# A soft mixture-of-experts layer: slot logits in three single-pass products instead of seven float32 products of halves

## The chip, the core and the metric

The kernel runs on one core of one Trainium2 chip as one program. The metric is device microseconds of that core from launch to end: 1880.38 us, the median of 3 runs (1880.1 to 1885.45). A core has a matrix engine (PE, with its weight loads PEld), a vector engine (DVE), an activation engine (ACT), a general engine (POOL), a sequencer that issues transfers (SP), an on-chip memory SBUF, and an accumulator memory PSUM that PE writes and DVE and ACT read. Each engine works through its own queue in order and waits on semaphores.

## The reference, cut to what matters

Four layers follow each other, each a graph convolution and a feed-forward part, on 625 nodes with 768 features. The change is in the feed-forward part of the third, `L2_ffn`, a soft mixture of 4 experts with 1024 slots each:

```python
x = x + _L2_ffn_ref(_layernorm(x, axis=-1)[None], phi, w1, b1, w2, b2)[0]

def _L2_ffn_ref(x, phi, w1, b1, w2, b2):
    logits = jnp.einsum('bnd,esd->bnes', x, phi)
    B, N, E, S = logits.shape
    dispatch = jax.nn.softmax(logits, axis=1)
    combine = jax.nn.softmax(logits.reshape(B, N, E * S), axis=-1).reshape(B, N, E, S)
    slots = jnp.einsum('bnd,bnes->besd', x, dispatch)
    h = jax.nn.gelu(jnp.einsum('besd,edh->besh', slots, w1) + b1[None, :, None, :])
    y = jnp.einsum('besh,ehd->besd', h, w2) + b2[None, :, None, :]
    return jnp.einsum('besd,bnes->bnd', y, combine)
```

The logits are one product of 4096 x 768 (phi) with 768 x 625 (x transposed). All inputs and outputs are float32.

## The kernel before

Nodes lie in 5 tiles of 125 (`TILES`), features in 6 blocks of 128 (`KD`). `x` (125 x 5 x 768) and the normalized, transposed `xT` (128 x 6 x 625, with a 626th column of zeros in `xTp`) stay in SBUF from stage to stage. Weights come through a pool `w` of 4 buffers, each filled by one transfer that SP issues (`weight`, L151). PSUM gives 4 tiles of 1024 columns in turn (`ps`, L89). The program is built by a scheduler that orders each engine's queue by dependences and priorities, so the order of the source is not quite the order of the queues.

`L2_ffn` has three parts.

First, x times w1 for the four experts, into `xw` (125 x 5 x 768): tile 0 by itself, then two pairs of tiles by `tile_pair`, which makes a 2 x 2 block product from seven block products (`right_sums` on DVE, `left_sums` on POOL). The last node tile is only normalized and turned while this runs (`turn_due`, called in `whole`). The bias row `br` is added on POOL (L1958).

Second, 16 *fronts*, `front(i)`, each making the logits of 256 slots (two blocks of 128) for all 625 nodes. phi is loaded 512 slots at a time. `half_nodes` makes sums of halves of xT once (DVE, partly in the place of xT). For each front `half_products` makes four sums of 128 x 384 from phi on POOL (L340 to L344), one front ahead, and `half_mm` runs seven products of halves, each 3 matmuls with 128 weight columns and 313 moving columns in float32; the results are combined by seven adds on DVE (L360) and one copy on ACT (L368). The two logit blocks of a front form a `pair` (128 x 2 x 625). `largest_slots(i)` then takes each slot's maximum over nodes, the exponentials `ex`, and the running maximum `M` over slots.

Between the products of a front other work of PE is interleaved by the three lists `c`: `turn` (five transposes of `ex`, copied from PSUM to `Dn` by DVE and ACT in alternation, `copy` L106) and `hidden` (five matmuls of `Dn` with `xw`, scaled on DVE into `hE`), both for the slots of the front before. In the second front after an expert's last one, `spread` puts the node maxima into `mrow`, `weights` subtracts them from the expert's four pairs on DVE (L1799) and takes exponentials on ACT (L1802), and `combine` multiplies the pairs with `hE` on PE (80 records) into `Z`, which lies where `xw` lay. So up to six pairs live at a time (`ltp`, 6 buffers).

Third, after the fronts, the last expert is finished, `Z` is scaled, turned and multiplied with w2 (`turn_sums`, `out`), and `out` adds the result to `x[:, t]` and hands the tile on to the next layer (`final`).

Of the kernel before, what the change touches and what calls it, by code (L numbers as in the profile page):

```python
# [8 lines left out]

F32 = mybir.dt.float32  # L10
BF16 = mybir.dt.bfloat16
F16 = mybir.dt.float16
I32 = mybir.dt.int32
AF = mybir.ActivationFunctionType
ALU = mybir.AluOpType
AX = mybir.AxisListType

N = 625
P = 125
NT = N // P  # L20
D = 768
KD = D // 128
# [2 lines left out]
FF = 192  # L25
NF = NEXP * FF // 128
BIG = 1e30
TILES = [slice(t * P, (t + 1) * P) for t in range(NT)]


def halves(r):

    return r.rearrange("p (h c) -> p h c", h=2)


class Net:
# [310 lines left out]
    def half_mm(self, pool, prods, top, bottom, between=((), (), ())):  # L347


        nc, HN, HK = self.nc, self.HN, self.HK  # L350
        pa, pb = self.ps(), self.ps()
        a1, a2 = pa[:, 0:HN], pa[:, 512 : 512 + HN]
        b1, b2 = pb[:, 0:HN], pb[:, 512 : 512 + HN]

        def prod(n, to):
            A, B = prods[n - 1]
            self.mm(to, [A[:, k, :] for k in range(HK)], [B[:, k, :] for k in range(HK)])

        def add(out, in0, in1):
            nc.vector.tensor_tensor(out, in0, in1, ALU.add)  # L360

        C11, C12, C21, C22 = (
            c[:, n] for c in (top, bottom) for n in (slice(0, HN), slice(HN, N))
        )
        U2 = pool.tile([128, HN], F32, tag="U2", name="U2", bufs=1)
        U3, w = C21, N - HN
        prod(1, a1)
        nc.scalar.copy(C11, a1)  # L368
        prod(6, a2)
        add(U2, C11, a2)  # L370
        prod(7, b1)
        add(U3, U2, b1)
        prod(5, b2)
        add(C22, U3[:, 0:w], b2[:, 0:w])
        add(C12, U2[:, 0:w], b2[:, 0:w])
        for f in between[0]:
            f()
        prod(4, a1)
        add(C21, U3, a1)
        for f in between[1]:  # L380
            f()
        prod(2, a2)
        add(C11, C11, a2)
        for f in between[2]:
            f()
        prod(3, b1)
        add(C12, C12, b1[:, 0:w])

    def half_begin(self, pool, prods, top):

# [1264 lines left out]
    def L2_ffn(self):  # L1655
        nc, tc, a, x = self.nc, self.tc, self.a, self.x
        NE, HF, NB = 4, 192, 8
        with ExitStack() as ctx:
            big = ctx.enter_context(tc.tile_pool(name="f2", bufs=1))


# [2 lines left out]
            f = big.tile([P, NT, NE], F32, name="f")  # L1664
# [3 lines left out]
            nc.gpsimd.memset(fp, 0.0)  # L1668
            with ExitStack() as c1:
                b1 = c1.enter_context(tc.tile_pool(name="f2e", bufs=1))  # L1670
                xw = b1.tile([P, NT, NE, HF], F32, name="xw")
                Z = xw
                xT = self.xT


                br = self.row(None, D, a["L2_ffn_b1"].rearrange("(o e) f -> o (e f)", o=1))
                ws = []
                for j in range(2):
                    w = self.wp.tile([128, KD, 2, HF], F32, tag="w", name="w1")
# [7 lines left out]
                with tc.tile_pool(name="f2x", bufs=1) as xp:  # L1687

                    ws = [w.rearrange("p k e f -> p k (e f)") for w in ws]
                    pv = self.hv(self.ps(), P)  # L1690
                    for j in range(2):
                        self.mm(
                            pv[:, j, :], [xT[:, k, TILES[0]] for k in range(KD)],
                            [ws[j][:, k, :] for k in range(KD)],
                        )
                    nc.vector.tensor_tensor(halves(xwf[0]), pv, halves(br), ALU.add)
                    HK = self.HK
                    rights = self.right_sums(
                        xp, [[w[:, k : k + HK, :] for w in ws] for k in (0, HK)]
                    )  # L1700
                    lefts = {1: self.left_sums(xp, xT, 1, inplace=False)}

                    def whole():
                        self.turn_due(NT - 1)
                        lefts[3] = self.left_sums(xp, xT, 3, inplace=False)

                    for t in (1, 3):
                        self.tile_pair(
                            xp, lefts[t], rights,
                            [xwf[o][:, js] for o in (t, t + 1) for js in (slice(0, 384), slice(384, D))],  # L1710
                            whole if t == 1 else None,
                        )
                ltp = c1.enter_context(tc.tile_pool(name="f2l", bufs=6))
                mp = c1.enter_context(tc.tile_pool(name="f2m", bufs=1))
                tp = c1.enter_context(tc.tile_pool(name="f2t", bufs=2))
                pairs, hEs, Ms, S = {}, {}, {}, {}
                ph, sts, exs, Dns, rows = {}, {}, {}, {}, {}

                B = self.half_nodes(b1, inplace=True)

                def sums_of_phi(i):
                    g, j = divmod(i, 2)
                    if j == 0:
                        ph[g] = self.weight(
                            a["L2_ffn_phiT"][:, g * 512 : (g + 1) * 512], KD, 512
                        )
                    S[i] = self.half_products(tp, B, ph[g], *(
                        slice((2 * j + o) * 128, (2 * j + o + 1) * 128) for o in range(2)
                    ))

                def front(i, *between):

                    pair = pairs[i] = ltp.tile([128, 2, N], F32, tag="lt", name="lt")
                    self.half_mm(tp, S.pop(i), pair[:, 0, :], pair[:, 1, :], between)

                def largest_slots(i):

                    e, q = divmod(i, NB // 2)
                    pair = pairs[i]
                    for o in range(2):  # L1740
                        st = sts[2 * i + o] = self.small.tile(
                            [128, 3], F32, tag="sm2", name="sm2", bufs=5
                        )
                        lt = pair[:, o, :]
                        nc.vector.tensor_reduce(st[:, 0:1], lt, AX.X, ALU.max, negate=True)
                        ex = exs[2 * i + o] = tp.tile([128, N], F32, tag="ex", name="ex")
                        nc.scalar.activation(
                            ex, lt, AF.Exp, bias=st[:, 0:1], accum_out=st[:, 1:2]
                        )
                    if q == 0:  # L1750
                        M = Ms[e] = mp.tile([128, N], F32, tag="M", name="M")
                        nc.vector.tensor_tensor(M, pair[:, 0, :], pair[:, 1, :], ALU.max)
                    else:
                        for o in range(2):
                            nc.vector.tensor_tensor(Ms[e], Ms[e], pair[:, o, :], ALU.max)

                def turn(i):
                    tv = self.nv(self.ps(), P, 128)
# [123 lines left out]
                def turn_sums(t, ks):  # L1882

                    if t not in zTs:
                        zT = ltp.tile([128, NK + 1, P], F32, tag="lt", name="zT")
                        zTs[t] = zT[:, 0:NK, :]
                        fTs[t] = zT[:96, NK, :].bitcast(BF16)[:, 0:P]
                    n = len(ks)
                    pv = self.ps()[:, 0:1024].rearrange("p (k c) -> p k c", c=128)[:, :, :P]
                    z = Z[:, t].rearrange("p e f -> p (e f)")  # L1890
                    for i, k in enumerate(ks):
                        nc.tensor.transpose(
                            pv[:, i, :], z[:, k * 128 : (k + 1) * 128], self.ident[:P, :P]
                        )
                    if ks[-1] < NK - 1:
                        nc.scalar.copy(zTs[t][:, ks[0] : ks[-1] + 1, :], pv[:, 0:n, :])
                        return
                    nc.scalar.copy(zTs[t][:, ks[0] : ks[-1] + 1, :], pv[:, 0:n, :])
                    nc.tensor.matmul(
                        pv[:96, n, :], fp[:, t].rearrange("p j r -> p (j r)"),  # L1900
                        self.identb[:P, :P], start=True, stop=True,
                    )
                    nc.vector.tensor_copy(fTs[t], pv[:96, n, :])

                def out(t, ks):
# [15 lines left out]
                            )  # L1921
                    if not last:
                        return
                    xv = halves(x[:, t, :])
                    nc.vector.scalar_tensor_tensor(
                        xv, pv, rs[:, t : t + 1], xv, ALU.mult, ALU.add
                    )
                    self.final(t)

# [29 lines left out]
                for i in range(LAST):  # L1959
# [14 lines left out]
                    if i == LAST - 1:  # L1974

                        turn(o)
                        turn(o + 1)
                    largest_slots(i)
                    if e >= 0 and q == 0:
                        largest(e)  # L1980
                    if e >= 0 and q == 1:
# [447 lines left out]
```

## Time and profile before

| What | Value |
|---|---|
| median of 3 runs | 1880.38 us |
| span of the profiled execution | 1877.8 us |
| mean granted PE clock | 0.985 of full |
| `L2_ffn`, 995.2 to 1394.0 us of the span | 398.8 us |
| of it x times w1, up to 1030.4 | 35.2 us, PE busy all of it |
| of it the fronts, up to 1322.9 | 292.5 us |
| of it the rest | 71.1 us, PE busy 67.94 |

The profiled execution is one run; its span goes from the first instruction to the last and lies 2.6 us under the median of the timed runs. In the timeline, a line is a group of like instructions: start, length, engine, line of the source, operation, tiles out<-in, shape and count, and in brackets how long the engine was idle before it and what ended that. A float32 matmul leaves two records, a float32 transpose one. The length of a PE record goes to the end of the pipeline, so successive records overlap; the time a matmul takes is read from start to start. The groups of sums that the change removes, over the fronts alone:

```
L340 POOL TENSOR_TENSOR S<-w 128x384 f32<-128x384 f32 x14 | 14.3, 1018 | 163.5 <-PE ps L125 163.5
L341 POOL TENSOR_TENSOR S<-S,w 128x384 f32<-128x384 f32 x14 | 14.0, 1001 | 1.1
L343 POOL TENSOR_TENSOR w<-w 128x384 f32<-128x384 f32 x14 | 21.9, 1564 | 0.0
L344 POOL TENSOR_TENSOR S<-w,S 128x384 f32<-128x384 f32 x14 | 19.8, 1414 | 0.0
```

Behind the count stand busy us and mean ns of one, then the idle time of the engine before them.

### The profile page before, as it was taken

What the parts mean: (1) busy time and instruction counts of PE and PEld (TensorE: products, weight loads), DVE (VectorE), ACT (ScalarE), POOL (GpSimd) and SP (SyncE); (2) the same over time, 40 slices, a digit from 0 to 9 for tenths busy, and PEclk for the clock granted to TensorE, in tenths of its full rate; (3) what the DMA queues carried; (4) which work ended last, traced back from release to release, by engine and by line L of the source; (5) the groups of instructions that cost most, each with busy time, mean ns of one, the idle gap of its engine ahead of it and who ended that gap; (6) DMA issues with size and microseconds to landing.
All of it is one profiled execution on the core that took longest, in us unless ns stands there. A gap on an engine that the chain in (4) does not pass through costs nothing.

```text
span 1877.8 us, 21626 instructions
## 1 busy us (share of the span) xinstructions
PE 1816.6 (97%) x8224; PEld 1268.2 (68%) x8224; DVE 1132.1 (60%) x2253; ACT 525.1 (28%) x950; POOL 649.7 (35%) x496
## 2 busy tenths in 40 slices
PE   8868899999999999999999999999999999999998
PEld 7835566556677766655555788878767888556765
DVE  8799856658566765675836464554756555144452
ACT  2468721002254533110110131322314333111200
POOL 0068665335410045743206322231235321401551
PEclk9959899999999999999999999999999999999999
DMA  2040033211200024414421211001011111021321
GB/s 70 25 143 34 19 110 99 79 59 36 87 22 26 1 70 150 132 51 148 135 67 37 73 62 40 26 26 34 6 40 46 39 63 67 1 80 46 99 68 33
DMA packets 69637, 115.03 MB, mean 61 GB/s; under 512 B 8189, under 2 KB 38111, under 8 KB 69534
## 3 DMA queue, kind: packets, MB, share of 16 engines
q1 hardware_dynamic: 69274, 113.57, 18.9%
q8 instruction: 65, 1.06, 0.2%
q14 instruction: 38, 0.31, 0.1%
q10 hardware_dynamic: 260, 0.09, 0.0%
HBM read 111.63 MB, written 2.01 MB: 61 GB/s over the span
## 4 chain that ended last, share of the span: by engine, by line
PE 86%; DVE 7%; ACT 3%; DMA 2%; issue 1%; SPq 0%; ACTq 0%; DVEq 0%
PE ps L125 68%; PE ps L118 3%; PE ps L1543 2%; PE ps L1575 2%; PE ps L1914 2%; PE ps L781 2%; DVE gat_w L595 2%; PE ps L1562 2%; DVE junk L575 2%; PE ps L189 1%; PE ps L1760 1%; DMA x<-in_x 1%; PE ps L132 1%; PE ps L719 1%; DVE av_junk L1380 1%
## 5 line engine op out<-in xcount | busy, mean ns | idle before, releaser
L340 POOL TENSOR_TENSOR S<-w 128x384 f32<-128x384 f32 x40 | 42.0, 1054 | 383.8 <-PE ps L125 281.7
L125 PE MATMUL ps<-xT,w 128*128 128x313 f32 x480 | 137.6, 427 | 0.7 <-ACT pr L1551 0.7
L565 POOL TENSOR_TENSOR gat_w<-gat_w,xT 125x625 f32<-125x625 f32 x60 | 86.1, 1469 | 119.7 <-DVE xT L537 97.6
L125 PE MATMUL ps<-w,xT 128*125 128x384 f32 (+2 forms) x392 | 125.3, 473 | 0.0
L125 PE MATMUL ps<-T,w 128*128 128x313 f32 x408 | 122.0, 430 | 0.8 <-DVE U L414 0.8
L125 PEld LDWEIGHTS ps<-xT,w 128*128 128x128 f32 x480 | 89.2, 189 | 33.6 <-ACT pr L1551 0.9
L125 PE MATMUL ps<-T,S 128*128 128x313 f32 x348 | 103.7, 431 | 1.7 <-DVE T L320 1.4
L125 PEld LDWEIGHTS ps<-w,xT 128*125 128x125 f32 x392 | 72.8, 188 | 46.4 <-issue 11.3
L125 PE MATMUL ps<-xT,S 128*128 128x313 f32 x336 | 100.8, 429 | 0.0
L125 PE MATMUL ps<-w,S 128*125 128x384 f32 x292 | 99.2, 486 | 0.0
L125 PEld LDWEIGHTS ps<-T,w 128*128 128x128 f32 x408 | 75.6, 189 | 31.9 <-issue 1.8
L125 PE MATMUL ps<-w,hg 128*125 128x384 f32 x288 | 96.3, 486 | 0.0
L125 PE MATMUL ps<-hh,gat_w 125*125 125x257 f32 (+1 forms) x400 | 89.8, 379 | 0.0
L125 PE MATMUL ps<-w,x2T 128*125 128x384 f32 (+1 forms) x280 | 84.2, 450 | 0.0
L125 PEld LDWEIGHTS ps<-T,S 128*128 128x128 f32 x348 | 63.9, 189 | 28.7 <-ACT lt L368 4.4
L125 PEld LDWEIGHTS ps<-w,S 128*125 128x125 f32 x292 | 54.7, 188 | 39.0 <-issue 0.7
L125 PEld LDWEIGHTS ps<-hh,gat_w 125*125 125x125 f32 x400 | 73.3, 187 | 11.3 <-issue 0.4
L125 PEld LDWEIGHTS ps<-xT,S 128*128 128x128 f32 x336 | 62.1, 189 | 24.2 <-DVE lt L360 1.7
L118 PE MATMUL ps<-gat_w,ft 125*65 125x500 f32 (+1 forms) x240 | 73.3, 463 | 5.2 <-DVE gat_w L595 3.0
L125 PEld LDWEIGHTS ps<-w,hg 128*125 128x125 f32 x288 | 53.6, 187 | 36.6 <-issue 0.6
L1380 DVE CUSTOM_DVE_ANT_0 av_junk<-av_w,av_a 128x512 f32<-128x512 f32 (+1 forms) x80 | 75.8, 947 | 3.1 <-DMA av_w<-in_L_gnn_W 1.0
L781 PE MATMUL ps<-ohd,ohs 125*125 125x313 bf16 x425 | 64.1, 304 | 9.0 <-DVE ohs L774 9.0
(460 smaller groups left out, 3804.6 us busy)
## 6 DMA issues: line engine op xcount, KB each, us to landing
w<-in_L_ffn_phiT SPq DMA_DIRECT2D x8, 1536.0 KB
w<-in_L_gnn_W SPq DMA_DIRECT2D x8, 1536.0 KB
gate<-gD SPq DMA_DIRECT2D x24, 312.5 KB
w<-in_L_ffn_w SPq DMA_DIRECT2D x6, 1152.0 KB
w<-in_L_gnn_W SPq DMA_DIRECT2D x6, 1152.0 KB
av_w<-in_L_gnn_W SPq DMA_DIRECT2D x24, 256.0 KB
av_w<-in_L_gnn_W SPq DMA_DIRECT2D x16, 384.0 KB
w<-in_L_ffn_w SPq DMA_DIRECT2D x3, 1536.0 KB
```

Of the source, the lines that this page charges most:

```text
L118: self.nc.tensor.matmul(pv[:, s, :], lhs[i], rhs[i][:, s, :], start=i == 0, stop=i == n - 1)
L125: self.nc.tensor.matmul(out, lhs[i], rhs[i], start=i == 0, stop=i == n - 1)
L340: nc.gpsimd.tensor_tensor(S1, A21, A22, ALU.add)
L565: nc.gpsimd.tensor_tensor(w[:, s, :], w[:, s, :], lc[:, s, :], ALU.add)
L575: nc.vector.tensor_tensor_reduce(self.n3(junk), row, self.n3(mb[:, t, :]), 1.0, -3e38, ALU.subtract, ALU.max, m[:, t : t + 1],)
L595: nc.vector.tensor_tensor(ws, ws, row.unsqueeze(1).to_broadcast(ws.shape), ALU.subtract)
L781: nc.tensor.matmul(acc[j // 2][:, j % 2, :], ohs[:, TILES[j]], ohd[:, 0:HN], start=c == cs[0], stop=c == cs[-1],)
L1380: nc.vector.tensor_tensor_reduce(junk, wt, row, 1.0, 0.0, ALU.mult, ALU.add, dst)
L1543: nc.tensor.matmul(sv[r][:, s, :], qk[half[r], 0, TILES[t]], self.n3(qk[half[r], 1, :])[:, s, :], start=True, stop=True,)
L1562: nc.tensor.transpose(tv[:, s, :], pr[:, s * P : (s + 1) * P], self.ident[:P, :P])
L1575: nc.tensor.matmul(ov[half[r]], v[:, s, h * DH : (h + 1) * DH], pT[r][:, s, :], start=s == 0, stop=s == NT - 1,)
L1914: nc.tensor.matmul(pv[:, j, :], zTs[t][:, k, :], w2[k // 3][:, k % 3, js], start=k == 0, stop=False,)
```

## The change

Each factor is split into a high part of 12 significant bits and a rest: phi into `high` and `low` with a third part `s` made of both, x into `xH`, `xM` (the rest, scaled by 2^12) and their sum `xS`. The logits are then `REST` times (high x xH + low x xM) plus s x xS: three products over all 768 features, without halves. The parts are typed float32r. A front is 2 slot blocks x 2 column parts (314 and 312 columns) x 18 matmuls: 6 into one PSUM bank, 12 into another, then a copy on ACT and one multiply-add on DVE.

The phi parts are made per slot block on ACT (`high`), POOL (`low`) and DVE (`s`) into buffers of the pool `w`; the x parts are made once, per node tile, on ACT and on POOL (tiles 0 to 2) or DVE (tiles 3, 4). In the built program phi's eight loads take one of the four buffers of `w` and the parts of the slot blocks the other three in turn.

The three parts of x need room. So x is written to DRAM (`xD`) at the start of the stage, `xw` and `Z` take its place in SBUF, and `out` reads each tile of x back into `xo`. Four buffers hold pairs, and three more pairs lie where xT lay (`room`). `largest_slots` runs per slot block, inside the front. `half_nodes`, `half_products` and `half_mm` are no longer called here.

```diff
+AWAY = 1.0 + 2.0**-13
+PART = 2.0**12
+REST = 1.0 - 2.0**-12
...
+    def split_weights(self, w, parts):
+        nc = self.nc
+        high, low, s = (parts[:, i] for i in range(3))
+        nc.scalar.activation(high, w, AF.Copy, scale=AWAY)
+        nc.gpsimd.tensor_tensor(low, high.bitcast(F32), w, ALU.subtract)
+        nc.vector.scalar_tensor_tensor(
+            s, high.bitcast(F32), 1.0 / PART, low.bitcast(F32), ALU.mult, ALU.subtract
+        )
+        return high, low, s
...
+            xD = dram.tile([P, NT, D], F32, name="xD")
...
-                xw = b1.tile([P, NT, NE, HF], F32, name="xw")
+                xw = x.rearrange("p t (e f) -> p t e f", e=NE)
...
+                xH, xM, xS = (
+                    b1.tile([128, KD, N + 1], F32R, name=n) for n in ("xH", "xM", "xS")
+                )
...
+                def split(t, eng):
+                    v, h, m, s = (m[:, :, TILES[t]] for m in (xT, xH, xM, xS))
+                    nc.scalar.activation(h, v, AF.Copy, scale=AWAY)
+                    eng.tensor_tensor(s, v, h.bitcast(F32), ALU.subtract)
+                    nc.scalar.activation(m, s.bitcast(F32), AF.Copy, scale=PART)
+                    eng.tensor_tensor(s, h.bitcast(F32), m.bitcast(F32), ALU.add)
...
+                for t in range(NT):
+                    nc.sync.dma_start(xD[:, t, :], x[:, t, :])
...
                         lefts[3] = self.left_sums(xp, xT, 3, inplace=False)
+                        for t in range(3):
+                            split(t, nc.gpsimd)
...
+                        if t == 1:
+                            for o in (3, 4):
+                                split(o, nc.vector)
-                ltp = c1.enter_context(tc.tile_pool(name="f2l", bufs=6))
+                ltp = c1.enter_context(tc.tile_pool(name="f2l", bufs=4))
+                flat = self.xTp.rearrange("p k c -> p (k c)")
+                room = {
+                    2 + r: flat[:, r * 2 * N : (r + 1) * 2 * N].rearrange("p (o c) -> p o c", o=2)
+                    for r in range(3)
+                }
...
-                B = self.half_nodes(b1, inplace=True)
...
-                    S[i] = self.half_products(tp, B, ph[g], *(
-                        slice((2 * j + o) * 128, (2 * j + o + 1) * 128) for o in range(2)
-                    ))
+                    w = ph[g][:, :, j * 256 : (j + 1) * 256]
+                    S[i] = [
+                        self.split_weights(
+                            w[:, :, o * 128 : (o + 1) * 128],
+                            self.wp.tile([128, 3, KD, 128], F32R, tag="w", name="parts"),
+                        )
+                        for o in range(2)
+                    ]
...
-                    pair = pairs[i] = ltp.tile([128, 2, N], F32, tag="lt", name="lt")
-                    self.half_mm(tp, S.pop(i), pair[:, 0, :], pair[:, 1, :], between)
+                    pair = pairs[i] = (
+                        room[i % 7] if i % 7 in room
+                        else ltp.tile([128, 2, N], F32, tag="lt", name="lt")
+                    )
+                    ks = range(KD)
+                    for o in range(2):
+                        high, low, s = S[i][o]
+                        for cs in (slice(0, 314), slice(314, N + 1)):
+                            n = cs.stop - cs.start
+                            p = self.ps()
+                            a, b = p[:, 0:n], p[:, 512 : 512 + n]
+                            to = pair[:, o, cs.start : min(cs.stop, N)]
+                            w = to.shape[1]
+                            self.mm(b, [s[:, k, :] for k in ks], [xS[:, k, cs] for k in ks])
+                            self.mm(
+                                a, [m[:, k, :] for m in (high, low) for k in ks],
+                                [m[:, k, cs] for m in (xH, xM) for k in ks],
+                            )
+                            u = tp.tile([128, 314], F32, tag="U2", name="U2")
+                            nc.scalar.copy(u[:, 0:w], b[:, 0:w])
+                            nc.vector.scalar_tensor_tensor(
+                                to, a[:, 0:w], REST, u[:, 0:w], ALU.mult, ALU.add
+                            )
+                            if o and not cs.start:
+                                for f in between[1]:
+                                    f()
+                        largest_slots(i, o)
+                        for f in between[2 * o]:
+                            f()
...
-                    xv = halves(x[:, t, :])
+                    xo = mp.tile([P, D], F32, tag="mrow", name="xo")
+                    nc.sync.dma_start(xo, xD[:, t, :])
                     nc.vector.scalar_tensor_tensor(
-                        xv, pv, rs[:, t : t + 1], xv, ALU.mult, ALU.add
+                        halves(x[:, t, :]), pv, rs[:, t : t + 1], halves(xo), ALU.mult, ALU.add
                     )
```

More of the change, by code (lines that the diff above doesn't have):

```diff
@@ L10 @@
 F32 = mybir.dt.float32
+F32R = mybir.dt.float32r
 BF16 = mybir.dt.bfloat16
@@ L1658, in L2_ffn @@
         with ExitStack() as ctx:
+            dram = ctx.enter_context(
+                tc.tile_pool(name="f2d", bufs=1, space=bass.MemoryType.DRAM)
+            )
+            xD = dram.tile([P, NT, D], F32, name="xD")
             big = ctx.enter_context(tc.tile_pool(name="f2", bufs=1))
@@ L1670, in L2_ffn @@
                 b1 = c1.enter_context(tc.tile_pool(name="f2e", bufs=1))
-                xw = b1.tile([P, NT, NE, HF], F32, name="xw")
+                xw = x.rearrange("p t (e f) -> p t e f", e=NE)
                 Z = xw
                 xT = self.xT
+                xH, xM, xS = (
+                    b1.tile([128, KD, N + 1], F32R, name=n) for n in ("xH", "xM", "xS")
+                )
+                for m in (xH, xM, xS):
+                    nc.gpsimd.tensor_copy(m[:, :, N:], self.xTp[:, :, N:])
+                def split(t, eng):
[4 more added lines that the diff above has]
+                    eng.tensor_tensor(s, h.bitcast(F32), m.bitcast(F32), ALU.add)
                 br = self.row(None, D, a["L2_ffn_b1"].rearrange("(o e) f -> o (e f)", o=1))
+                for t in range(NT):
+                    nc.sync.dma_start(xD[:, t, :], x[:, t, :])
                 ws = []
@@ L1726, in sums_of_phi @@
                         )
-                    S[i] = self.half_products(tp, B, ph[g], *(
-                        slice((2 * j + o) * 128, (2 * j + o + 1) * 128) for o in range(2)
-                    ))
-                def front(i, *between):
-                    pair = pairs[i] = ltp.tile([128, 2, N], F32, tag="lt", name="lt")
-                    self.half_mm(tp, S.pop(i), pair[:, 0, :], pair[:, 1, :], between)
-                def largest_slots(i):
+                    w = ph[g][:, :, j * 256 : (j + 1) * 256]
@@ new lines, in sums_of_phi @@
+                    S[i] = [
[5 more added lines that the diff above has]
+                    ]
+                def front(i, *between):
+                    pair = pairs[i] = (
[20 more added lines that the diff above has]
+                                to, a[:, 0:w], REST, u[:, 0:w], ALU.mult, ALU.add
+                            )
+                            if o and not cs.start:
[4 more added lines that the diff above has]
+                            f()
@@ L1738, in largest_slots @@
+                def largest_slots(i, o):
                     e, q = divmod(i, NB // 2)
                     pair = pairs[i]
-                    for o in range(2):
+                    for o in (o,):
                         st = sts[2 * i + o] = self.small.tile(
@@ L1749, in largest_slots @@
                         )
-                    if q == 0:
+                    if o and q == 0:
                         M = Ms[e] = mp.tile([128, N], F32, tag="M", name="M")
                         nc.vector.tensor_tensor(M, pair[:, 0, :], pair[:, 1, :], ALU.max)
-                    else:
-                        for o in range(2):
-                            nc.vector.tensor_tensor(Ms[e], Ms[e], pair[:, o, :], ALU.max)
+                    elif q:
+                        nc.vector.tensor_tensor(Ms[e], Ms[e], pair[:, o, :], ALU.max)
                 def turn(i):
@@ L1884, in turn_sums @@
                     if t not in zTs:
-                        zT = ltp.tile([128, NK + 1, P], F32, tag="lt", name="zT")
+                        zT = tp.tile([128, NK + 1, P], F32, tag="ex", name="zT")
                         zTs[t] = zT[:, 0:NK, :]
@@ L1977, in L2_ffn @@
                         turn(o + 1)
-                    largest_slots(i)
                     if e >= 0 and q == 0:
```

## The prediction

> **What bounds the kernel now.** I read the page's busy row, the page's chain, then the timeline of the logits stage of layer 2.
>
> ```profile
> PE 1816.6 (97%) x8224; PEld 1268.2 (68%) x8224; DVE 1132.1 (60%) x2253; ACT 525.1 (28%) x950; POOL 649.7 (35%) x496
> PE 86%; DVE 7%; ACT 3%; DMA 2%; issue 1%; SPq 0%; ACTq 0%; DVEq 0%
> 1030.40:1322.90 292.50, 292.07 (x1391) 234.46 (x1390) 150.66 (x273) 73.21 (x121) 72.69 (x60) 1.00 0.13 42
> ```
>
> The last line is the stage that is changed, 16 fronts long (PE, PEld, DVE, ACT, POOL busy, clock, DMA). PE is busy 292.07 of 292.50 us at clock 1.00; DVE is busy half of it, ACT and POOL a quarter. So PE time taken out is span taken out, until another engine is late. One front on PE (start, us, records):
>
> ```profile
> 1089.92 1.74 PE L125 MATMUL ps<-xT,w 128*128 128x313 f32 x6
> 1091.50 1.75 PE L125 MATMUL ps<-T,w 128*128 128x313 f32 x6
> 1093.08 0.49 PE L1760 MATMUL ps<-ident,ex 128*125 128x128 f32 x3
> 1093.60 1.85 PE L125 MATMUL ps<-T,S 128*128 128x313 f32 x6
> ...
> 1099.47 1.79 PE L125 MATMUL ps<-xw,Dn 125*128 125x192 f32 x10
> 1101.10 1.75 PE L125 MATMUL ps<-xT,w 128*128 128x313 f32 x6
> ...
> 1105.89 0.27 PE L1787 MATMUL ps<-ident,M 128*125 128x128 f32 x1
> ```
>
> One product of halves is three matmuls, six records, and starts 1.58 us before the next (1089.92 to 1091.50): 527 ns a matmul. The front takes 15.97 us: seven products 11.06, two `turn` (5 records of 109 ns each, 1.09), two `hidden` (1099.47 to 1101.10: 1.63 each, 3.26), and 0.56 in which products wait for the sums of the products before them.
>
> **What the change takes from PE.** Now 72 matmuls a front (2 slot blocks x 2 column parts x 18), 314 or 312 columns, in float32r, a type that no row shows. The bounds: above, a float32 matmul, 527 ns; below, the one-pass matmul of the same width:
>
> ```profile
> 29.40 1.50 PE L781 MATMUL ps<-ohd,ohs 125*125 125x313 bf16 x10
> 30.73 1.04 PE L719 MATMUL ps<-wb,xT 128*125 128x260 f32 x4
> ```
>
> Ten in 1.33 us: 133 ns. 527 is four times 132, so float32 looks like four passes. I take 133, the row whose passes the program asks for. The weight load has to hide: a load of float32 weights is 189 ns long in the rows, but the 128-column transposes of 109 ns each carry one, so loads can come every 109 ns. A front's products are then 72 x 0.133 = 9.58 us, 1.48 less: 23.7 over 16 fronts. The 0.56 of waits inside a front also goes (each new group waits only for a buffer): 0 to 9.0 over 16 fronts, I take 5.
>
> The Trainium skill (FP8 and Floating Point Precision, TensorE Precision Notes) says that reduced-precision float32 is read in 4 bytes and cut to about 22 bits, and true float32 takes four passes; the four passes agree with the 527 ns. Against the change speaks TensorE: Matmul & The Clock Gate, LDWEIGHTS: a load takes its columns / 1.2, 107 ns for 128, an estimate that leaves 26 ns of each 133 ns product free where float32 left far more. If the load were added instead of hidden, the products would take 72 x 240 ns and the kernel lose some 95 us.
>
> **What it adds, and where it lies.** Per front: ACT gets two `high` (128x768; `ACTIVATE` 128x625 is 0.81, 128x1250 1.25, so 0.91 each) and three more copies of 0.41; POOL changes four sums of 128x384 (1.00 to 1.57) for two `low` of 128x768 (1.81, the row of 125x768 at L1958); DVE loses seven adds of 0.48 and gets four of 0.48 and two `s` of 128x768 (1.02 with an operand in PSUM, L1305; 0.95 at L449): +0.5. The sums leave all three under 12 us of a front of 14.5, so throughput is not the limit. Order is: the parts of a front have three buffers, so each second part is split in the middle of the front before, and DVE has `s` in its queue ahead of work that PE waits for. I followed the built order of the changed kernel through four places.
>
> (a) The start. Layer 2 now splits x: five times two ACT (0.9) and two 128x750 on POOL (1.8 alone) or DVE. On ACT's queue the square root of node tile 4's layer norm stands behind `xM` of tile 1, so behind POOL's queue.
>
> ```profile
> 996.14 1.97 POOL L471 TENSOR_TENSOR S<-xT 128x375 f32<-128x375 f32 x1
> 998.26 1.92 DVE L450 TENSOR_TENSOR Td<-Td,w 128x1152 f32<-128x1152 f32 x1
> 1002.38 1.06 DVE L182 TENSOR_SCALAR xn<-x,lt_mv,lt_r 125x768 f32<-125x768 f32 x1
> 1006.82 0.81 PE L189 MATMUL ps<-ident,xn 125*128 125x125 f32 x6
> ```
>
> Tile 4 is normalized at 1002.4, four microseconds before PE turns it at 1006.5. Afterwards: POOL's three sums end at 998.9 as now, the first split sum doubles beside DVE's L450/L451 (3.4 us, 1002.3), two sums of 1.0 (1004.4), the next split sum 1.8 (1006.2); ACT `xM`, `xH`, square root 2.1 (1008.3); DVE reciprocal, a split of 0.9 to 1.4, `xn` 0.9 (1010.6 to 1011). PE waits 4.5 us (2 to 6). Left sums for the second tile pair come later too, but PE is as late.
>
> (b) The second front. Of the four weight buffers three now hold parts, so phi's loads (1536 KB, two fronts' worth) have one, and the next starts only when POOL has read the last part of the old one. A load's bytes have come 6 us after its issue (windows; the last two columns are DMA share and GB/s):
>
> ```profile
> 1054.95 0.38 SPq L154 DMA_DIRECT2D w<-in_L_ffn_phiT  x1
> 1059.50:1061.00 1.50, 1.50 (x7) 1.08 (x6) 1.50 (x3) 1.42 (x3) 1.50 (x2) 1.00 0.80 309
> 1061.00:1062.50 1.50, 1.47 (x8) 1.03 (x7) 1.50 (x3) 0.60 (x3) 1.50 (x2) 1.00 0.02 8
> ```
>
> From front 0's start, the last part's `low` ends at 7.5, phi lands at 13.6, `high`, `low`, `s` end at 17.4, and the copy `Dn` behind `s` on DVE at 18.2; PE wants it at 17.9. With queue delays 2 us (0 to 3). Later loads have half a front more and cost ACT a wait of some 1.5 us that no PE work stands behind. The five stores of x (375 KB each) stand on SP's queue behind phi's first load and ahead of the second, which is due over 30 us later: nothing. Five reads of x at the end are issued when `mrow` is free, 12 us apart, ahead of an add that needs them: nothing; 3 us each if that cover fails.
>
> (c) The three fronts that also weigh an expert (`spread`, `weights`). Now DVE copies `Dn` first:
>
> ```profile
> 1111.09 0.82 DVE L109 COPY Dn<-ps 125x640 f32<-125x640 f32 x1 [0.39 <-PE ps L1760]
> 1111.83 1.45 DVE L1799 TENSOR_TENSOR lt<-lt,mrow 128x1250 f32<-128x1250 f32 x1
> ```
>
> Afterwards the order on DVE is add, `s`, maximum, M, two subtractions, `Dn`. From the front's start: the second part's buffer is free at 4.8 (36 x 133 ns), `high` 5.7, `low` 7.6, `s` 8.6, maximum 9.4, M 10.2, subtractions 13.0, `Dn` 13.8. PE has done its spread, both turns and the third group at 8.9 and wants `Dn` for `hidden`: 5 us lost (3 to 7). In the middle one of the three the copy on DVE is the second turn's, wanted later: 2 us (1 to 4). Together 12 (7 to 18).
>
> (d) The last front's turns: 1 us (0 to 2).
>
> **The sum.** -23.7 - 5 + 4.5 + 2 + 12 + 1 = -9.2 us. The profiled span is 1877.8 and the median 1880.38, 2.6 more; against the median 1871.
>
> **The rivals.** First, full gain: the waits of (a) to (c) find slack that I don't see: -23.7 - 5 + 2, 1854. For it: PE is gapless now; against it: the queue orders are fixed. Chance 0.10.
>
> Second, slower: splitting sets the pace. POOL and DVE slow each other when both read two SBUF tensors:
>
> ```profile
> 1060.27 1.57 POOL L343 TENSOR_TENSOR w<-w 128x384 f32<-128x384 f32 x1
> 1061.01 1.49 DVE L1755 TENSOR_TENSOR M<-M,lt 128x625 f32<-128x625 f32 x1
> ```
>
> Alone they are 1.00 and 0.86. If `low` takes 3.6 and `s` 1.7 (these ratios and 2.0 of (a)), an ordinary front's chain of 4.8 + 0.9 + 5.3, maximum, M, add ends past 13.4, when PE wants that PSUM buffer: 0.7 us x 13 fronts, 2.3 x 3 in (c), 3 in (a): +19, 1890. It decides from `low` + `s` = 5 us; I have 2.8, since DVE mostly sits waiting while `low` runs. Chance 0.20, its milder half about no change. The Trainium skill (GPSIMD Engine Reference, Specifications) states this contention for DVE instructions with two SBUF inputs, as the rows show; by it alone, without the order, all of `low` would be slow and this rival would be the forecast.
>
> Third, float32r isn't one pass. Each ns over 133 costs 1.15 us: from 141 ns nothing is gained. At 263 (two passes) a front's products take 18.9 us, +126, with (b) to (d) hidden: about 2000. Only the type's missing row speaks for it. Chance 0.10.
>
> **How the numbers follow.** The forecast, 1862 to 1880, has 0.60. This kernel's runs tell 0.3% (5.6 us) from no change: faster is under 1874.7. Forecast 0.48 of 0.60 and full gain 0.10 make faster 0.58; the forecast's rest 0.12 and the milder half of the second rival 0.09 make same 0.21; 0.21 slower. Bounds of all terms: -23.7 - 9 + 9 = 1857 at the low end, -23.7 + 29 plus 4 ns a matmul (137, what the bf16 rows reach) = 1890 at the high end.
>
> **What would show it.** Right: groups of 36 float32r matmuls start to start in 4.8 us; PE gaps at `hidden` waiting for DVE `Dn` in three fronts, and one of 2 to 6 us ahead of tile 4's transposes. Wrong: matmuls above 141 ns; `low` above 2.5 us; PE idle in ordinary fronts; gaps in the last 70 us on the reads of x.

## The result, and the profile after

The changed kernel takes 1888.75 us, the median of 5 runs (1887.45 to 1890.3), beside 1880.38 of the kernel before: ratio 1.0039, 95% interval 1.0026 to 1.0051. It is slower by 0.4%, outside the 0.3% named as no change. The forecast was 1871, faster, with a chance of 0.60 for 1862 to 1880; the time lies above that and inside the bounds of all terms (1857 to 1890): slower where faster was forecast. The profiled executions give the same difference: 1885.7 against 1877.8 us, 7.9 more.

The page's busy row and the row of its chain by engine:

```profile
PE 1805.0 (96%) x8704; PEld 1314.4 (70%) x8704; DVE 1141.5 (61%) x2237; ACT 576.6 (31%) x1040; POOL 638.6 (34%) x473
...
PE 30%; DVE 1%; ACT 1%; issue 0%; ACTq 0%
```

The chain is followed back through only 32% of the span here, to 1278 us, so it says little of this stage. Busy time in the fronts by windows (stretch, length, then PE, PEld, DVE, ACT and POOL busy with counts, PE clock, DMA share, GB/s):

```profile
1038.48:1327.40 288.92, 275.85 (x1845) 274.70 (x1844) 152.31 (x251) 114.58 (x196) 59.52 (x34) 0.98 0.16 53
```

PE lost 11.6 us of busy time over the whole kernel, and yet the span grew. The fronts now hold 13 us in which PE is idle, and the mean clock of the stretch is 0.98 where it was 1.00. (The windows of fronts before and after don't end at the same work; below, both are taken to the last `hidden`.)

An ordinary stretch of a front on PE:

```profile
1089.11 0.71 PE L1839 MATMUL ps<-ident,ex 128*125 128x128 f32 x5
1089.66 1.79 PE L134 MATMUL ps<-x,Dn 125*128 125x192 f32 x10
1091.15 1.16 PE L134 MATMUL ps<-xS,parts 128*128 128x312 f32 x6
1092.15 1.03 PE L134 MATMUL ps<-xH,parts 128*128 128x312 f32 x6
1093.01 1.04 PE L134 MATMUL ps<-xM,parts 128*128 128x312 f32 x6
1093.89 1.79 PE L134 MATMUL ps<-x,Dn 125*128 125x192 f32 x10
```

There is no gap here. Six float32r products start 0.86 to 0.88 us before the next group (1092.15 to 1093.01 to 1093.89), so one takes 143 to 147 ns, and the median over all is 145: 5.2 us for 36, not 4.8. That is above the 141 ns from which, by the prediction, nothing is gained.

The start of the stage on ACT, DVE and PE (timeline):

```profile
1008.46 0.28 ACT L182 ACTIVATE lt_r<-lt_mv,eps 125x1 f32<-125x1 f32 x1
...
1008.86 2.37 DVE L1709 TENSOR_TENSOR xS<-xT,xH 128x750 fp32r<-128x750 f32 x1
1011.15 2.13 DVE L191 TENSOR_SCALAR xn<-x,lt_mv,lt_r 125x768 f32<-125x768 f32 x1
...
1013.43 1.48 PE L198 MATMUL ps<-ident,xn 125*128 125x125 f32 x6 [6.36 <-DVE xn L191]
```

The square root starts at 1008.46, where the prediction's chain has it end at 1008.3. Behind it the two DVE instructions take 4.5 us instead of some 2, while POOL is busy without a break beside them. PE waits 6.36 us, and its transposes then take twice their usual time: the clock.

The second front and the first front that weighs an expert, on DVE and PE:

```profile
1056.68 2.56 DVE L405 SCALAR_TENSOR_TENSOR parts<-parts 128x768 fp32r<-128x768 f32 x1 [2.31 <-POOL parts L404]
1059.17 0.81 DVE L118 COPY Dn<-ps 125x640 f32<-125x640 f32 x1
...
1060.04 1.89 PE L134 MATMUL ps<-x,Dn 125*128 125x192 f32 x10 [1.76 <-DVE Dn L118]
...
1119.08 0.96 DVE L405 SCALAR_TENSOR_TENSOR parts<-parts 128x768 fp32r<-128x768 f32 x1 [1.13 <-POOL parts L404]
1119.96 0.80 DVE L1825 TENSOR_REDUCE sm<-lt 128x1 f32<-128x625 f32 x1
1120.67 0.80 DVE L1834 TENSOR_TENSOR M<-M,lt 128x625 f32<-128x625 f32 x1
1121.39 2.83 DVE L1878 TENSOR_TENSOR lt<-lt,mrow 128x1250 f32<-128x1250 f32 x2
1124.13 0.82 DVE L118 COPY Dn<-ps 125x640 f32<-125x640 f32 x1
...
1125.10 3.02 PE L134 MATMUL ps<-x,Dn 125*128 125x192 f32 x10 [4.67 <-DVE Dn L118]
```

Read the second part from top to bottom: `Dn`, for which PE waits, stands behind `s`, the maximum, M and both subtractions, the order that the prediction gave. And ten records of `hidden` are 3.02 us long there, 1.79 in the ordinary front. The windows of the clock (PE clock is the third figure from the end) say why:

```profile
1013.43:1016.20 2.77, 2.77 (x9) 2.15 (x10) 2.77 (x2) 1.22 (x2) 1.50 (x1) 0.50 0.00 0
1122.00:1125.10 3.10, 0.01 (x1) 0.04 (x1) 3.10 (x4) 3.09 (x6) 0.00 (x0) 1.00 0.00 0
1125.80:1129.00 3.20, 3.20 (x13) 3.20 (x12) 2.77 (x4) 2.54 (x3) 0.00 (x0) 0.50 0.03 5
1280.60:1286.00 5.40, 5.40 (x18) 5.40 (x19) 3.46 (x5) 3.60 (x4) 0.00 (x0) 0.50 0.00 0
```

Behind each long wait PE works at half clock, for 3.0, 3.4 and 5.5 us by windows of 1 us (those shown lie inside these stretches), and so loses half of that again: 1.5, 1.7 and 2.7 us. Summed up, from trace to trace:

| Term | Forecast | Measured | Read from |
|---|---|---|---|
| products | -23.7 | -9.9 | 1152 x 145 ns against 112 x 1.58 us |
| (a) start | +4.5 | +8.0 | stage up to the fronts 8.0 longer: gap 6.36, nearly all the rest half clock |
| (b) second front | +2 | +1.8 | gap 1.76 |
| (c) weighing fronts | +12 | +15.7 | gaps 4.67, 0.67 + 1.30, 4.67; half clock 1.7 + 2.7 |
| (d) last turns | +1 | +1.0 | gap 1.03 |
| gaps of before in this stretch | 0 | -0.5 | 0.53 in its trace (298.69 less 298.16 busy) |
| waits inside fronts | -5 | -7.3 | not read for itself: what remains of 298.7 against 299.5 us |
| from the last `hidden` on | 0 | -0.9 | 64.95 against 64.03 us |
| sum | -9.2 | +7.9 | |

So of the 17 us between forecast and result 13.8 are the price of a product, and 7 are waits and the clock behind them; the rest, 3.7, goes the other way.

### The profile page after: what moved, and what is told of

It reads as the page before. It is cut to its first block, busy times and chain, and to the rows that moved or that the text cites. A ratio compares the mean times of both kernels' runs of the same rounds, so it can differ in the third digit from the quotient of the medians.

```text
span 1885.7 us, 22661 instructions
## 1 busy us (share of the span) xinstructions
PE 1805.0 (96%) x8704; PEld 1314.4 (70%) x8704; DVE 1141.5 (61%) x2237; ACT 576.6 (31%) x1040; POOL 638.6 (34%) x473
## 5 line engine op out<-in xcount | busy, mean ns | idle before, releaser
L404 POOL TENSOR_TENSOR parts<-parts,w 128x768 fp32r<-128x768 f32 x32 | 59.3, 1855 | 211.8 <-ACT parts L403 211.8
L349 POOL TENSOR_TENSOR S<-w 128x384 f32<-128x384 f32 x24 | 24.6, 1031 | 219.0 <-PE ps L134 116.9
L134 PE MATMUL ps<-xT,w 128*128 128x313 f32 x288 | 81.7, 428 | 0.7 <-ACT pr L1572 0.7
L134 PE MATMUL ps<-T,S 128*128 128x313 f32 x252 | 74.2, 427 | 1.4 <-DVE T L329 1.4
L134 PE MATMUL ps<-x,Dn 125*128 125x192 f32 x320 | 60.2, 339 | 13.4 <-DVE Dn L118 11.1
L134 PE MATMUL ps<-xS,parts 128*128 128x312 f32 (+1 forms) x384 | 72.4, 325 | 0.0
L134 PEld LDWEIGHTS ps<-w,x2T 128*125 128x125 f32 x280 | 52.2, 188 | 26.6 <-issue 0.2
L596 DVE CUSTOM_DVE_ANT_0 junk<-ps,mb 125x625 f32<-125x625 f32 x85 | 68.4, 804 | 3.7 <-PE ps L141 1.4
L134 PEld LDWEIGHTS ps<-xT,w 128*128 128x128 f32 x288 | 53.9, 189 | 21.9 <-ACT pr L1572 0.9
```

Of the source, the lines that this page charges most:

```text
L134: self.nc.tensor.matmul(out, lhs[i], rhs[i], start=i == 0, stop=i == n - 1)
L349: nc.gpsimd.tensor_tensor(S1, A21, A22, ALU.add)
L404: nc.gpsimd.tensor_tensor(low, high.bitcast(F32), w, ALU.subtract)
L596: nc.vector.tensor_tensor_reduce(self.n3(junk), row, self.n3(mb[:, t, :]), 1.0, -3e38, ALU.subtract, ALU.max, m[:, t : t + 1],)
```

## The experiments

### e1: the start, and what came of its gain

```diff
                     eng.tensor_tensor(s, v, h.bitcast(F32), ALU.subtract)
+                    if t < 3:
+                        nc.scalar.copy(m[:, 0, 0:1], xT[:, 0, TILES[4]][:, 0:1])
                     nc.scalar.activation(m, s.bitcast(F32), AF.Copy, scale=PART)
```

> The scaled part xM of tiles 0 to 2 is given a dependence on the turned tile 4 (one element is copied from it first), so that the square root of tile 4's layer norm stands ahead of xM on ACT's queue. Theory (the wait at the start is ACT's queue order, and the PE clock of 0.5 after it belongs to the wait): the PE gap of 6.36 us ahead of tile 4's transposes goes, and with it the half clock until 1016.2, 1.6 us more; 1888.75 - 8.0 = 1880.7 us (1879 to 1882.5). Rival (the splits on POOL set the pace of this stage, so another wait takes its place, at the left sums or at the first front's parts): less than 3 us gained, 1886 to 1889.

Measured: 1885.4 us, ratio to the kernel before 1.0029 (1.0018 to 1.0040). Only 3.3 us are gained. The timeline of PE of this kernel, then windows behind its last line and behind the long waits of the first and the last weighing front (4.38 and 4.67 us):

```profile
994.74 11.78 PE L134 MATMUL ps<-w,xT 128*125 128x384 f32 x36
1006.36 0.81 PE L198 MATMUL ps<-ident,xn 125*128 125x125 f32 x6
...
1029.93 1.33 PE L134 MATMUL ps<-xS,parts 128*128 128x314 f32 x6
...
1053.09 2.92 PE L134 MATMUL ps<-x,Dn 125*128 125x192 f32 x10 [3.38 <-DVE Dn L118]
```

```profile
1053.90:1057.00 3.10, 3.10 (x12) 3.10 (x12) 2.60 (x6) 1.49 (x3) 0.00 (x0) 0.50 0.00 0
1119.79:1125.40 5.61, 5.61 (x19) 5.61 (x20) 3.47 (x5) 3.60 (x4) 0.00 (x0) 0.50 0.01 3
1276.39:1282.40 6.01, 6.01 (x21) 6.01 (x22) 3.47 (x5) 3.60 (x4) 0.00 (x0) 0.50 0.00 0
```

The theory of the place is right: the wait and its half clock are gone, and the fronts start 8.55 us earlier, at 1029.93 (0.55 of it because the stage does, at 994.74 against 995.29). The theory of the time is wrong, because the rival is right about what follows: the second front's wait for `Dn` grows from 1.76 to 3.38 us and now halves the clock too, 3.2 us of the gain together. A wait taken away on one path came back on the next, dearer for the clock. Some 1.4 us more are clock too: behind the long waits of the weighing fronts the half clock lasts 5.6 and 6.0 us of work here, 3.4 and 5.5 in the changed kernel. That leaves 3.4 of the 8.0 us, near the 3.3 measured.

### e2: the order in the weighing fronts

```diff
+                    if 0 < i < LAST - 1:
+                        c[0] += [(turn, o)]
+                        c[1] += [(turn, o + 1), (hidden, o)]
+                        c[2] += [(hidden, o + 1)]
                     if e >= 0 and q == 1:
                         c[0] += [(spread, e), (weights, e, 0), (weights, e, 1)]
                         c[1] += [(weights, e, 2)]
                         c[2] += [(weights, e, 3)]
-                    if 0 < i < LAST - 1:
...
```

> In the three fronts that weigh an expert, the turn of a slot block is put ahead of the spread and the subtractions in program order; nothing else. Theory (Dn's copy is late because it stands behind the subtractions on DVE): both PE gaps of 4.67 us and the half clock behind each (1.6 and 2.7 us) go, -13.6; about 1.3 us comes back in two fronts where the second turn's copy on ACT stands behind the exponentials; 1888.75 - 11 = 1878 us (1875 to 1881). Rival (DVE's work in these fronts is too much for their length, whatever its order): the wait moves to the sums of the products, 3 us gained at most, 1886 us or more.

Measured: 1877.59 us, ratio 0.9994 (0.9984 to 1.0003); 11 us less than the changed kernel, as expected. PE in the first weighing front of this kernel:

```profile
1119.74 0.98 PE L134 MATMUL ps<-x,Dn 125*128 125x192 f32 x5
1120.41 1.16 PE L134 MATMUL ps<-xS,parts 128*128 128x312 f32 x6
1121.41 1.03 PE L134 MATMUL ps<-xH,parts 128*128 128x312 f32 x6
1122.28 1.04 PE L134 MATMUL ps<-xM,parts 128*128 128x312 f32 x6
1124.89 1.89 PE L134 MATMUL ps<-x,Dn 125*128 125x192 f32 x10 [1.57 <-ACT Dn L120]
```

The first `hidden` no longer waits. The second waits 1.57 us for the copy on ACT, and its ten records take 1.89 us: after so short a wait the clock is full (1.00 in the window from 1125 to 1128). DVE had room for this work; only its order was against it.

### e3: the third part off DVE

```diff
-        nc.vector.scalar_tensor_tensor(
-            s, high.bitcast(F32), 1.0 / PART, low.bitcast(F32), ALU.mult, ALU.subtract
-        )
+        nc.scalar.activation(s, high.bitcast(F32), AF.Copy, scale=1.0 / PART)
+        nc.gpsimd.tensor_tensor(s, s.bitcast(F32), low.bitcast(F32), ALU.subtract)
```

> The third part s of phi is made on ACT (scaling) and POOL (difference) in place of one instruction on DVE. Theory (s delays Dn on DVE's queue): the gap of 1.8 us in the second front goes, and the waits in the three weighing fronts are 1 us shorter each; 1888.75 - 5 = 1884 us (1882 to 1886), with POOL and ACT far from full. Rival (a phi part's chain of high, low, s sets the pace, and it is longer now by 0.85 + 1.85 - 1.0 us): PE waits for parts in fronts, 1890 us or more.

Measured: 1876.55 us, ratio 0.9978 (0.9969 to 0.9988): 12 us gained where 5 were expected. DVE in its first weighing front:

```profile
1116.39 0.48 DVE L1805 SCALAR_TENSOR_TENSOR lt<-ps,U 128x311 f32<-128x311 f32 x1 [0.96 <-ACT U L1804]
1116.79 0.81 DVE L118 COPY Dn<-ps 125x640 f32<-125x640 f32 x1
1117.52 0.79 DVE L1824 TENSOR_REDUCE sm<-lt 128x1 f32<-128x625 f32 x1
1118.23 2.32 DVE L1833 TENSOR_TENSOR M<-M,lt 128x625 f32<-128x625 f32 x1
1120.47 2.82 DVE L1877 TENSOR_TENSOR lt<-lt,mrow 128x1250 f32<-128x1250 f32 x2
```

The expectation left the rest of the queue as it was. But the scheduler, with `s` gone, put `Dn` directly behind the add, ahead of the maximum, M and the subtractions. So the waits of 4.67 us went with it, beside the one in the second front; waits of 1.71, 1.56 and 1.69 us remain in the three weighing fronts. The rival, a longer chain of a part setting the pace, is refuted here: POOL is busy 64.5 us longer for it over the kernel (703.1 against 638.6), and PE waits for no part in the fronts. What it costs shows in the fourth line: M, which reads two tensors in SBUF beside POOL, takes 2.32 us (0.80 in the same front of the changed kernel).

### p1: what a product costs

Added after the last front, each group twelve times, results unused:

```diff
+                for k, n in enumerate((64, 128, 192, 256, 314, 384, 448, 512)):
+                    probe(k, n)
+                probe(8, 314, 64)
+                probe(9, 314, 32)
...
```

> After the last front 14 groups of 12 matmuls each are added, whose results are not used: float32r with 64, 128, 192, 256, 314, 384, 448 and 512 moving columns and 128 weight columns; 314 moving columns with 64 and with 32 weight columns; 314 with the same weights and the same moving data in all twelve; the same data as float32; as bfloat16 read from the upper halves of the 4-byte words; bfloat16 packed. Read from start to start. Theory 1 (a fixed cost per float32r product): columns / 2.4 + 14 ns, 41 ns at 64 and 227 at 512, whatever the weights. Theory 2 (each column costs more): 0.46 ns a column, 30 at 64 and 236 at 512. Theory 3 (the load of the weights shows): flat near 145 up to 314 columns, and near 133 with 32 or 64 weight columns. The bfloat16 rows near 133, the float32 row near 527.

Three records each of the groups with 314 and 512 columns in the timeline; the time of one is read from start to start:

```profile
1335.54 0.31 PE L2071 MATMUL ps<-xM,parts 128*128 128x314 f32 x1
1335.68 0.31 PE L2071 MATMUL ps<-xH,parts 128*128 128x314 f32 x1
1335.83 0.31 PE L2071 MATMUL ps<-xM,parts 128*128 128x314 f32 x1
...
1343.08 0.40 PE L2071 MATMUL ps<-xM,parts 128*128 128x512 f32 x1
1343.32 0.40 PE L2071 MATMUL ps<-xH,parts 128*128 128x512 f32 x1
1343.55 0.39 PE L2071 MATMUL ps<-xM,parts 128*128 128x512 f32 x1
```

Median start to start, without the first and the last of the twelve, at clock 1.00:

| Product | ns |
|---|---|
| float32r, 64 / 128 / 192 columns | 112 / 111.5 / 111 |
| float32r, 256 / 314 / 384 / 448 / 512 columns | 119.5 / 145.5 / 176 / 203.5 / 233 |
| float32r, 314 columns, 64 / 32 weight columns | 143.5 / 143.5 |
| float32r, 314 columns, same weights and data each time | 146 |
| float32, 314 columns | 2 x 264 |
| bfloat16, 314 columns, upper halves of 4-byte words | 140.5 |
| bfloat16, 314 columns, packed | 133 |

Theory 2 holds from 256 columns on: 0.45 to 0.47 ns for each column, and no fixed part of 14 ns (theory 1 wants 227 at 512, and 41 at 64). Below that there is a floor of 111 ns. The weights don't make the 145: with a quarter of them it is 143.5. The Trainium skill (TensorE: Matmul & The Clock Gate, LDWEIGHTS) has columns / 1.2 for a load, an estimate of 107 ns for 128; the floor of 111 agrees with it, though no group with fewer weight columns was run below 314 moving columns to show that the load is the floor. If it is, the warning weighed in the prediction binds products under some 240 columns (111 / 0.46, an estimate) and not these. The same page (Back-to-back issue gap) has columns / 2.4 + 2.5 ns for a product by itself at full clock, an estimate of 133.3 at 314: the packed bfloat16 row agrees, the float32r row is 12 ns above. More than half of the 12 appears in bfloat16 as soon as both operands are read from every second place (140.5). The packed group also has the same data in all twelve, but in float32r that changes nothing (146). What the rest is stays open.

### e4: the three edits together

> The three edits of e1, e2 and e3 together. Theory: e3 took the waits on DVE's queue (12 us), the second front's among them, which in e1 grew and ate half of what the earlier start had given; so here the earlier start arrives whole: 1876.55 - 8.3 = 1868 us (1866 to 1870.5), with gaps of about 1.6 us left in the three weighing fronts, where the second turn's copy stands behind the exponentials on ACT. Rival (POOL, which now also makes s, is late for the first fronts because the bias sums stand in its queue): the start is given back, 1873 us or more.

Measured: 1868.4 us, ratio 0.9935 (0.9923 to 0.9947). The gains that ate each other alone add up here, and the rival (POOL late for the first fronts) is not seen; at the start PE waits 0.93 us for DVE instead. The weighing fronts keep waits of 1.45, 1.26 and 1.43 us.

### e5: e4 with the weighing over two fronts

```diff
                     if e >= 0 and q == 1:
-                        c[0] += [(spread, e), (weights, e, 0), (weights, e, 1)]
-                        c[1] += [(weights, e, 2)]
-                        c[2] += [(weights, e, 3)]
+                        c[0] += [(spread, e)]
+                        c[1] += [(weights, e, 0)]
+                        c[2] += [(weights, e, 1)]
+                    if e >= 0 and q == 2:
+                        c[0] += [(weights, e, 2)]
+                        c[1] += [(weights, e, 3)]
...
-                    if e >= 0 and q == 1:
+                    if e >= 0 and q == 2:
                         combine(e)
```

> e4, with the weighing of an expert spread over two fronts and its combine one front later (seven pairs then live, as many as there is room for). Theory: the last 1.6 us gap goes in each of the three weighing fronts: e4 - 4.8, 1863 us (1861 to 1866). Rival (the exponentials and subtractions are as much in the way in the next front): as e4, 1868 us.

Measured: 1863.49 us as expected, ratio 0.9913 (0.9899 to 0.9927): 0.9% faster than the kernel before, the best of the kernels that keep the logits fine. Its profiled execution was its longest (1870.44 us; the stage and its fronts begin 6 us later than in e4), so only the fronts are read from it:

```profile
1038.34:1310.87 272.53, 271.48 (x1851) 271.06 (x1850) 136.76 (x222) 135.85 (x227) 122.62 (x64) 1.00 0.17 57
```

PE is busy all but 1.1 us and at full clock. The window ends 0.73 us into the last turn; up to the end of the last product, where the changed kernel's window ends, the fronts take 271.8 us, 17.1 less than there.

### b1: e5 with a cheaper product

All three products of the fronts read bfloat16 upper halves; the logits are coarse.

```diff
+                            top = lambda v: v.bitcast(BF16)[:, 1::2]
...
-                            self.mm(b, [s[:, k, :] for k in ks], [xS[:, k, cs] for k in ks])
+                            self.mm(
+                                b, [top(s[:, k, :]) for k in ks], [top(xS[:, k, cs]) for k in ks]
+                            )
...
```

> e5, with the three products reading only the upper two bytes of each 4-byte word, as bfloat16: the same addresses, loads and order, but 10 to 12 significant bits fewer, so the logits are coarse. Theory (PE's price of a product sets these fronts, 145 ns in float32r and 140.5 in this form): 1152 x 4.5 ns, 5.2 us under e5, 1858 us. Rival (something else paces the fronts): within 1.5 us of e5.

Measured: 1859.54 us, 4.0 under e5, a little short of the 5.2 expected. The runs of e5 lie up to 8 us apart and those of b1 up to 4, so the size is not sharp. In the traces PE's work from the first front to the last `hidden` falls from 280.3 to 274.7 us, 5.5: each nanosecond of a product is still paid in full there, as the prediction had it (1.15 us).

## Why the prediction was wrong

- **The step that failed** is "I take 133, the row whose passes the program asks for". float32r does not come at the price of packed bfloat16: p1 and the fronts show 145 ns at 314 columns, near the one pass assumed and far from two (263). With 1152 products that is 13.8 us, and it alone turns -9.2 into +4.6. The prediction named the threshold (141 ns) and held its third rival at 0.10 with the argument that only a missing row speaks for it. A type without a row is itself the reason for a wide bound: the high end allowed 137.
- **(a)** The mechanism was right, the square root behind `xM` on ACT's queue, and e1 shows it. The size was off: 0.9 to 1.4 and 0.9 us were put down for two DVE instructions that take 2.37 and 2.13 beside POOL. The second rival quotes that effect for instructions that read two tensors in SBUF, as the split does; `xn` reads one, and was slowed as well (0.68 at 990.64, with POOL idle). The clock was not thought of. A small misreading went with it: PE turns tile 4 at 1006.82 in the row shown, not at 1006.5.
- **(b)** Right in place, 1.8 against 2, but the size is in part luck: the chain put `s` at 1.0 us and found 0.3 before "queue delays"; in the trace `s` takes 2.56 beside POOL, and that 1.6 is nearly the whole wait of 1.76. That it was held small by lateness elsewhere was not seen: after e1 it is 3.4.
- **(c)** The chain was right to the instruction in the first and the last of the three fronts, and their gaps of 4.67 us met the forecast of 5. In the middle one PE waits 0.67 us for `rm`, which the chain did not have, and 1.30 us at the second `hidden`, which the trace puts down to ACT's exponentials (L1881); DVE's `Dn`, which the prediction named, ends 0.15 us before PE starts, so which of the two it was stays open. All gaps are 11.3 us against 12; the clock behind them, 4.4 us, makes the term too small. In e2 and e3 `Dn` comes ahead of the subtractions by two different edits and the long waits go, which confirms the cause.
- **(d) and x in DRAM**: right. The trace shows no wait of an engine for `xo`, and the last stretch is 0.9 us shorter. The waits inside fronts went as said, some 7 us as a remainder against 5.
- **The rivals.** Splitting as the pace: refuted, `low` is 1.86 us in the mean, and with 64.5 us more work on POOL PE waits for no part (e3). Full gain: right only in that all waits could be ordered away. The third had the right place, in a milder form than the two passes for which its time was worked out.
- **The sum** took the waits as fixed. With most of them ordered away (e5) the kernel is 17 us under the kernel before. That misses the first rival's 1854 by 9.5 us, less than the 13.8 that the products cost more than was put down.

## What to carry to other kernels

Where a change puts an instruction form on the bounding engine that no row shows, its price times its count is the largest unknown of the sum; compute from what price on nothing is gained, and give the case beyond it a chance in proportion. A change that shortens the bounding engine's work uncovers the queue order of the others: follow what stands ahead of each instruction that PE waits for, expect waits removed one at a time to reappear at the next place, and judge the edits together. A long wait of PE can cost more than its length: those of 3.38 us and more cost 1.5 to 3.0 us on top here, because the clock behind them was halved; those of up to 1.8 us did not.

## What the runs showed of the hardware

- **Clock after a wait.** Waits of 1.3 to 1.8 us left the clock at 1.00. After 3.38, 4.38, 4.67 and 6.36 us (changed kernel and e1) it was 0.50 for 3.0 to 6.0 us of work, which adds 1.5 to 3.0 us to a wait. In the changed kernel the clock falls at 1009.58, 1125.6 and 1279.2 us and rises at 1016.4, 1129.0 and 1286.0 (windows of 1 us): all lie multiples of 3.41 us apart, wherever the wait began, so that two waits of 4.67 us have 3.4 and 5.5 us of half clock behind them. The Trainium skill (TensorE: Matmul & The Clock Gate, Part 1) says that an idle window of about 3.4 us halves the clock and a busy one of that length restores it, with the window running freely; the spacing fits it. But PE need not be idle for a whole window: at the start the clock fell some 2.5 us after PE stopped (1007.07 to 1009.58).
- **float32r** costs 0.45 to 0.47 ns a column from 256 columns on, with a floor of 111 ns at 64 to 192 columns, and 3.6 times less than float32 (527 to 145) rather than 4 times.
- **bfloat16 read from every second place** is slower than packed, 140.5 against 133 ns at 314 columns.
- **DVE beside POOL.** A split instruction of 128x750 took 2.37 us beside POOL and 0.93 with POOL idle; `s` of 128x768 2.56 and 0.96.
